# Layer 1's elu as max(min(exp(h), 1), h + 1), with h + 1 from the product with W, in a four-layer graph kernel planned by a list scheduler

## Chip, cores, metric

One core of a Trainium2 chip. The jobs ran on several chips, so each kernel is compared with the kernel before on the same chip. The metric is device microseconds of an execution, the median of several. Each run also has a profile of one execution. Ratios are computed as the mean time of one kernel's runs over the mean of the other's runs of the same rounds, so they are not quite the ratio of the medians that are quoted.

## The reference, cut to what matters

`x` is 64 x 256 x 128 in fp32, `adj` a 256 x 256 matrix of zeros and ones that all graphs share. Four graph layers follow one another, each as `x = layernorm(x + layer(x))`. The change is in the last line of layer 1:

```python
def _L1_gnn_ref(x, adj, W, a_src, a_dst):
    h = jnp.einsum('bnf,fo->bno', x, W)
    ...                                   # attention weights attn from h, a_src, a_dst, adj
    h_prime = jnp.einsum('bij,bjo->bio', attn, h)
    return jax.nn.elu(h_prime)            # h if h > 0, else exp(h) - 1
...
x = _layernorm(x + _L1_gnn_ref(...), axis=-1)
```

Layer 2 is a gated recurrence of five steps and holds most of the matmuls.

## The kernel before

The kernel works on 32 units of two graphs each; seven are under way at a time, in seven "lanes" of buffers. Every instruction is first a task in a plan: engine, planned nanoseconds, a function that issues it, the cells it reads and writes. A list scheduler then simulates the five engines with the planned durations and fixes one order for every engine; the program issues that order, with semaphores between the engines. In the trace of the kernel before, the source lines of TensorE, VectorE and ScalarE follow one another as in the built program (1079, 2310 and 1033 stretches of equal lines).

```python
LATENCY = {"pe": 700, "dve": 600, "act": 600, "pool": 700, "sp": 4000}
...
add(DVE, 230, lambda: nc.vector.tensor_copy(wx1.ap[:, 0:D], ps_w1.ap[:, 0:D]), (ps_w1,), (wx1,))
add(DVE, 60, lambda: nc.vector.memset(wx1.ap[:, D : D + 1], 1.0 / D), (), (wx1,))
... # layer 1, per unit; hp is the product divided by the softmax sums, 128 x 512
add(DVE, 330, lambda: nc.vector.tensor_scalar_min(hn.ap, hp.ap, 0.0), (hp,), (hn,))
add(ACT, 550, lambda: nc.scalar.activation(th.ap, hn.ap, AF.Tanh, scale=0.5), (hn,), (th,))
add(ACT, 550, lambda: nc.scalar.activation(exf, hn.ap, AF.Exp), (hn,), (ex,))
xf = X[u].ap.rearrange("p b c d -> p (b c d)")
add(DVE, 600, lambda: nc.vector.scalar_tensor_tensor(hp.ap, hp.ap, 0.0, xf, op0=ALU.max, op1=ALU.add),
    (hp, X[u]), (hp,))
add(DVE, 600, lambda: nc.vector.scalar_tensor_tensor(th.ap, exf, 1.0, th.ap, op0=ALU.add, op1=ALU.mult),
    (ex, th), (th,))
add(DVE, 600, lambda: nc.vector.tensor_add(hp.ap, hp.ap, th.ap), (hp, th), (hp,))
layernorm(u, L, y_pairs(hp))
```

It computes exp(m) - 1, with m = min(h, 0), as (exp(m) + 1) * tanh(m / 2): three VectorE operations of 512 columns, one cheaper minimum and two ScalarE functions per unit.

The softmax here doesn't subtract the row's maximum and nothing guards it: scores larger than these inputs give would overflow.

## Time and profile before

| | before |
|---|---|
| median of 3 runs | 1464.49 us (1464.2 to 1466.8) |
| profiled span | 1463.0 us |
| TensorE busy | 1431.2 us, 98% |
| VectorE busy | 1101.1 us, 75% |
| ScalarE busy | 723.2 us, 49% |

TensorE's line is the one that bounds; the others are read for what they make TensorE wait for. The prediction below shows the lines themselves.

To see where TensorE loses time I also use a number that the page does not print. In an unbroken stream at full clock successive matmuls of this trace start 0.429 us apart at 512 columns, 0.216 us at 256 and 0.109 to 0.114 us at 128 to 133; at half clock, the 256-column ones start 0.427 us apart. Each start-to-start distance in the trace, less this pitch, is **lost time**: waits, half clock, and the many small hitches that "busy" hides. The pitches of all 5733 matmuls add up to 1415.9 us; the rest of a span is lost time (about 44 us) and the 2.8 us before the first matmul.

### The profile page before, as it was taken

The numbers are of one execution on the slowest core, as the hardware profiler recorded it, in microseconds if no ns is written. First come the engines' busy times: TensorE is split into PE (matmuls) and PEld (weight loads), VectorE is DVE, ScalarE is ACT, GpSimd is POOL, SyncE is SP. The second block draws the span as 40 slices with busy tenths as digits, with TensorE's granted clock in tenths as the row PEclk, the third lists the DMA queues.
The fourth block names the chain that finished last, engine by engine and source line by source line (L and its number), as shares of the span: only waits on it lengthen the run. The fifth ranks groups of instructions, "written<-read, shape, count | busy, mean of one in ns | idle before, by whom it ended". The sixth has DMA issues, their size and how long they took to land.

```text
span 1463.0 us, 18345 instructions
## 1 busy us (share of the span) xinstructions
PE 1431.2 (98%) x5733; PEld 967.9 (66%) x5733; DVE 1101.1 (75%) x2569; ACT 723.2 (49%) x1372; POOL 146.2 (10%) x134
## 2 busy tenths in 40 slices
PE   7899999999999999999999999999999999999998
PEld 6666666666667766577666666676666766665667
DVE  6884778868769788777886778977976877767565
ACT  4664446446354465444554545535554554544431
POOL 0110101100011101001010011111100100001011
PEclk9899999999999999999999999999999999999999
DMA  6211243453534444534435344344343334443212
GB/s 148 46 37 22 65 96 86 95 110 78 116 80 95 104 98 87 118 74 99 104 80 108 78 109 100 84 92 107 72 98 85 89 89 99 93 101 70 46 44 65
DMA packets 495280, 126.90 MB, mean 87 GB/s; under 512 B 443856, under 2 KB 465104, under 8 KB 495184
## 3 DMA queue, kind: packets, MB, share of 16 engines
q1 hardware_dynamic: 495184, 125.73, 38.7%
q8 instruction: 46, 0.75, 0.2%
q14 instruction: 50, 0.41, 0.1%
HBM read 71.41 MB, written 54.25 MB: 86 GB/s over the span
## 4 chain that ended last, share of the span: by engine, by line
PE 93%; DVE 3%; ACT 2%; DMA 1%; issue 0%; SPq 0%; DVEq 0%; ACTq 0%
PE ps L678 45%; PE ps L658 22%; PE ps L747 8%; PE ps L754 4%; PE ps L620 3%; PE ps L590 3%; PE ps L523 2%; PE ps L634 2%; PE ps L585 2%; PE ps L721 1%; ACT e L609 1%; PE ps L430 0%; DVE e L554 0%; DVE st L483 0%; DMA rowu<-cu 0%
## 5 line engine op out<-in xcount | busy, mean ns | idle before, releaser
L678 PE MATMUL ps<-m,gT 128*128 128x512 f32 x960 | 460.9, 593 | 3.6 <-ACT m L674 3.6
L678 PEld LDWEIGHTS ps<-m,gT 128*128 128x128 f32 x960 | 177.7, 190 | 152.8 <-issue 126.4
L488 POOL TENSOR_TENSOR rstd<-ve,nhalf 128x4 f32<-128x4 f32 x128 | 145.5, 1139 | 1311.5 <-DVE ve L485 1268.9
L658 PE MATMUL ps<-adjTp,ht 128*128 128x256 f32 x928 | 231.7, 381 | 1.8 <-DMA ht<-hb 1.5
L658 PEld LDWEIGHTS ps<-adjTp,ht 128*128 128x128 f32 x928 | 174.5, 191 | 74.4 <-issue 50.1
L697 DVE TENSOR_TENSOR p<-p,xT 128x512 f32<-128x512 f32 x160 | 109.6, 686 | 95.3 <-ACT p L691 95.0
L674 ACT COPY m<-ps 128x512 f32<-128x512 f32 x160 | 93.4, 584 | 174.0 <-PE ps L658 170.1
L684 ACT ACTIVATE e<-ps,bias 128x512 f32<-128x512 f32 x160 | 109.8, 686 | 133.9 <-PE ps L678 133.8
L693 ACT ACTIVATE e<-ps,bias 128x512 f32<-128x512 f32 x160 | 109.7, 686 | 117.0 <-PE ps L678 116.7
L678 PE MATMUL ps<-xT,gT 128*128 128x512 f32 x320 | 161.4, 594 | 3.1 <-DVE xT L700 3.1
L686 DVE SCALAR_TENSOR_TENSOR e<-e,xT 128x512 f32<-128x512 f32 x160 | 109.2, 684 | 72.4 <-ACT e L684 70.9
L678 PE MATMUL ps<-e,u5T 128*128 128x512 f32 x320 | 161.9, 592 | 0.0
L691 ACT ACTIVATE p<-ps,bias 128x512 f32<-128x512 f32 x160 | 109.7, 686 | 77.9 <-PE ps L678 74.0
L658 PE MATMUL ps<-adjT,x 128*128 128x256 f32 x512 | 132.2, 383 | 0.0
L658 PEld LDWEIGHTS ps<-adjT,x 128*128 128x128 f32 x512 | 95.8, 192 | 42.6 <-issue 32.0
L698 DVE SCALAR_TENSOR_TENSOR p<-e,p 128x512 f32<-128x512 f32 x160 | 109.5, 685 | 2.8 <-ACT e L693 0.4
L700 DVE SCALAR_TENSOR_TENSOR xT<-p,xT 128x512 f32<-128x512 f32 x160 | 109.5, 685 | 2.0
L483 DVE BATCH_NORM_STATS2 st<-ps 128x6 f32<-128x256 f32 x128 | 53.7, 426 | 57.5 <-PE ps L754 38.9
L678 PEld LDWEIGHTS ps<-e,u5T 128*128 128x128 f32 x320 | 59.2, 190 | 51.1 <-issue 40.7
L609 ACT ACTIVATE e<-m,esd 128x256 f32<-128x256 f32 x120 | 87.0, 761 | 2.1 <-DMA m<-row 2.1
L678 PEld LDWEIGHTS ps<-xT,gT 128*128 128x128 f32 x320 | 59.1, 190 | 41.8 <-issue 31.0
L708 DVE STREAM_TRANSPOSE p<-xT 128x512 f32<-128x512 f32 x116 | 81.6, 705 | 1.4
(135 smaller groups left out, 1861.2 us busy)
## 6 DMA issues: line engine op xcount, KB each, us to landing
hb<-p SPq DMA_DIRECT2D x174, 256.0 KB, 2.1
ht<-hb SPq DMA_DIRECT2D x464, 64.0 KB, 2.5
m<-row SPq DMA_DIRECT2D x60, 256.0 KB, 3.7
xT<-hb SPq DMA_DIRECT2D x232, 64.0 KB, 2.5
out_dram<-x SPq DMA_DIRECT2D x32, 256.0 KB, 2.4
z<-in_x_dram SPq DMA_DIRECT2D x100, 64.0 KB, 2.4
z<-in_x_dram SPq DMA_DIRECT2D x7, 256.0 KB, 4.2
u<-rowu SPq DMA_DIRECT2D x60, 3.8 KB, 3.0
```

The source lines that it names most:

```text
L488: add(POOL, 1050, lambda: nc.gpsimd.tensor_tensor(rstd.ap, ve.ap, nhalf.ap, op=ALU.pow), (ve, nhalf), (rstd,))
L609: add(ACT, 600, lambda g=g, b=b: nc.scalar.activation(e.ap[:, g, :].rearrange("p (c n) -> p c n", c=NC), ev()[:, b], AF.Prelu, bias=esd.ap ...
L658: add(PE, mm_ns(N), lambda b=b, mc=mc: nc.tensor.matmul(ps.ap[:, b * N : (b + 1) * N], lhs(b, mc), mat.ap[:, mc, :], start=(mc == 0), stop ...
L678: add(PE, mm_ns(T), lambda: nc.tensor.matmul(ps.ap, w(), rhs.ap, start=start, stop=stop, skip_group_check=True), (c, rhs), (ps,))
L684: add(ACT, 600, lambda ps_g=ps_g: nc.scalar.activation(r.ap, ps_g.ap, AF.Tanh, bias=bias2.ap[:, 1:2], scale=0.5), (ps_g, bias2), (r,))
L686: add(DVE, 600, lambda h=h: nc.vector.scalar_tensor_tensor(r.ap, r.ap, 1.0, h.ap, op0=ALU.add, op1=ALU.mult), (r, h), (r,))
L691: add(ACT, 600, lambda ps_v=ps_v: nc.scalar.activation(v.ap, ps_v.ap, AF.Tanh, bias=bias2.ap[:, 2:3]), (ps_v, bias2), (v,))
L693: add(ACT, 600, lambda ps_g=ps_g: nc.scalar.activation(z.ap, ps_g.ap, AF.Tanh, bias=bias2.ap[:, 0:1], scale=0.5), (ps_g, bias2), (z,))
L697: add(DVE, 600, lambda h=h: nc.vector.tensor_sub(v.ap, v.ap, h.ap), (v, h), (v,))
L698: add(DVE, 600, lambda: nc.vector.scalar_tensor_tensor(v.ap, z.ap, 1.0, v.ap, op0=ALU.add, op1=ALU.mult), (v, z), (v,))
L700: add(DVE, 600, lambda h=h, new=new: nc.vector.scalar_tensor_tensor(new.ap, v.ap, 0.5, h.ap, op0=ALU.mult, op1=ALU.add), (v, h), (new,))
L747: add(PE, mm_ns(N), lambda k=k, src=src, c=c, b=b: nc.tensor.matmul(view(c)[:, :, b, :], bn(src.ap)[:, b, c * P : (c + 1) * P], w3.ap[:, k ...
```

## The change

Write h for the value that goes into the elu (h_prime in the reference). The product with W that makes h gets 1/D added to every entry of W. The rows of layer 1's input sum to D there (the kernel already adds 1 to each element of the normalized input), so the product, divided by the softmax sums, is h + 1 without an instruction more, and `hp` holds it. The exp takes off the 1 again with a bias of -1. Then elu(h) + 1 = max(min(exp(h), 1), h + 1), and the 1 left over drops out in the layernorm that follows. Per unit one VectorE minimum, one VectorE 512-wide operation and one ScalarE tanh go.

```diff
+    minus1 = cell("minus1", [P, 1])
+    add(DVE, 60, lambda: nc.vector.memset(minus1.ap, -1.0), (), (minus1,))
...
-    add(DVE, 230, lambda: nc.vector.tensor_copy(wx1.ap[:, 0:D], ps_w1.ap[:, 0:D]), (ps_w1,), (wx1,))
+    add(DVE, 230, lambda: nc.vector.tensor_scalar_add(wx1.ap[:, 0:D], ps_w1.ap[:, 0:D], 1.0 / D), (ps_w1,), (wx1,))
...
-        add(DVE, 330, lambda: nc.vector.tensor_scalar_min(hn.ap, hp.ap, 0.0), (hp,), (hn,))
-        add(ACT, 550, lambda: nc.scalar.activation(th.ap, hn.ap, AF.Tanh, scale=0.5), (hn,), (th,))
-        add(ACT, 550, lambda: nc.scalar.activation(exf, hn.ap, AF.Exp), (hn,), (ex,))
+        add(ACT, 550, lambda: nc.scalar.activation(exf, hp.ap, AF.Exp, bias=minus1.ap), (hp, minus1), (ex,))
         xf = X[u].ap.rearrange("p b c d -> p (b c d)")
-        add(DVE, 600, lambda: nc.vector.scalar_tensor_tensor(hp.ap, hp.ap, 0.0, xf, op0=ALU.max, op1=ALU.add),
-            (hp, X[u]), (hp,))
-        add(DVE, 600, lambda: nc.vector.scalar_tensor_tensor(th.ap, exf, 1.0, th.ap, op0=ALU.add, op1=ALU.mult),
-            (ex, th), (th,))
-        add(DVE, 600, lambda: nc.vector.tensor_add(hp.ap, hp.ap, th.ap), (hp, th), (hp,))
+        add(DVE, 600, lambda: nc.vector.scalar_tensor_tensor(hp.ap, exf, 1.0, hp.ap, op0=ALU.min, op1=ALU.max),
+            (ex, hp), (hp,))
+        add(DVE, 600, lambda: nc.vector.tensor_add(hp.ap, hp.ap, xf), (hp, X[u]), (hp,))
```

The list scheduler sees fewer tasks, and from about 57 us on every engine's queue has another order.

More of the change, by code (lines that the diff above doesn't have):

```diff
@@ L623, in layer1 @@
         add(ACT, 500, lambda: nc.scalar.copy(px.ap, ps_x.ap), (ps_x,), (px,))
-        rs, hp, hn, th = L["rs"], L["ht"], L["m"], L["xT1"]
+        rs, hp = L["rs"], L["ht"]
         ex = L["h0"]
```

## The prediction

> **What bounds the kernel now.** I read the page's busy table first, then its slices, then the waits of TensorE, then 2 us windows of the first 90 us, then VectorE's and TensorE's timelines where TensorE stood still.
>
> The busy table and the slices (one digit is the busy tenths of 1/40 of the span):
> ```profile
> PE 1431.2 (98%) x5733; PEld 967.9 (66%) x5733; DVE 1101.1 (75%) x2569; ACT 723.2 (49%) x1372; POOL 146.2 (10%) x134
> ...
> PE   7899999999999999999999999999999999999998
> ...
> PEclk9899999999999999999999999999999999999999
> ```
> TensorE is busy 98% of 1463.0 us and every slice but the first two and the last is at 9. Busy alone could hide slack[...], so I checked the pace: the chain has 8 matmuls of L678 in 3.43 us, 429 ns each for 512 columns, and 16 of L658 in 3.45 us, 216 ns for 256. The same 0.84 ns a column from both sizes is a stream without gaps. The change does not remove a matmul, so nothing below 1431 us is in reach, and at most 1463.0 - 1431.2 = 31.8 us (2.2%) is to be had, from TensorE's idle time. Where that lies, from the waits of TensorE:
> ```profile
> PE ps L430 <- DVE x L497: 4.7, 1, 4.7
> PE ps L473 <- DVE esd L595: 4.2, 2, 3.2
> PE ps L678 <- ACT m L674: 3.6, 3, 1.8
> PE ps L678 <- DVE xT L700: 3.1, 2, 1.9
> ...
> PE ps L620 <- DVE p L613: 2.2, 1, 2.2
> PE ps L658 <- DMA ht<-hb: 1.5, 2, 1.3
> ```
> The columns are total, times and longest, in us. By time: 4.4 us waiting for the first loads, 11.5 us between 28 and 57 us (the first units' layers 0 and 1, with too few units under way to fill TensorE), 9.0 us in eight short waits of at most 1.9 us from 212 to 1229 us, and about 6.7 us after the last matmul. Layer 1's elu lies ahead of the longest one, L430 <- L497: L430 transposes unit 0's layer-1 output, L497 writes it. In 2 us windows (busy us of PE, PEld, DVE, ACT, POOL, then granted clock):
> ```profile
> 50.00:52.00 2.00, 2.00 (x20) 1.99 (x18) 2.00 (x7) 0.78 (x4) 1.01 (x1) 1.00 0.00 0
> 52.00:54.00 2.00, 0.19 (x2) 0.00 (x0) 2.00 (x8) 1.15 (x2) 0.03 (x1) 1.00 0.00 0
> 54.00:56.00 2.00, 0.00 (x0) 0.00 (x0) 2.00 (x9) 0.00 (x0) 0.98 (x1) 0.55 0.04 1
> 56.00:58.00 2.00, 1.16 (x4) 0.88 (x5) 2.00 (x8) 0.00 (x0) 0.00 (x0) 0.50 0.04 12
> 58.00:60.00 2.00, 2.00 (x7) 1.52 (x6) 2.00 (x9) 0.00 (x0) 1.82 (x2) 0.50 0.38 119
> 60.00:62.00 2.00, 2.00 (x12) 1.78 (x11) 2.00 (x10) 1.22 (x3) 0.30 (x1) 0.74 0.02 4
> ```
> Here VectorE, full in every window, is the bound; TensorE stands idle from 52.2 to 56.8 us and then runs at half clock until about 61 us.
>
> [...]after 4.65 us of idleness the clock was 0.50, and L658 pairs took 1.06 us in place of 0.60; the 1.9 us waits later left it at 1.00. [...]the trace has 681 to 688 ns on L646, L648 and L650, whatever the operations are, so a min with a max in one instruction should cost the same.[...]
>
> **The change part by part.** The layer-1 group rows of before:
> ```profile
> L646 DVE SCALAR_TENSOR_TENSOR ht<-ht,x 128x512 f32<-128x512 f32 x32 | 22.0, 687 | 0.5
> L648 DVE SCALAR_TENSOR_TENSOR xT<-h,xT 128x512 f32<-128x512 f32 x32 | 21.8, 682 | 1.3 <-ACT h L644 1.1
> L650 DVE TENSOR_TENSOR ht<-ht,xT 128x512 f32<-128x512 f32 x32 | 21.8, 681 | 0.3
> ...
> L642 DVE TENSOR_SCALAR m<-ht 128x512 f32<-128x512 f32 x32 | 13.5, 422 | 0.5
> ...
> L643 ACT ACTIVATE xT<-m 128x512 f32<-128x512 f32 x32 | 20.1, 627 | 15.7 <-DVE m L642 15.5
> L644 ACT ACTIVATE h<-m 128x512 f32<-128x512 f32 x32 | 19.8, 618 | 0.0
> ```
> There are 32 units. *VectorE* loses the min (13.5 us) and one of three 512-wide operations (21.8 us): 35.3 us, so about 1066 us busy. *ScalarE* loses the tanh (20.1 us)[...]: net -17 us, about 706 us. *TensorE* keeps the same matmuls. The added constant is one 60 ns memset; the added scalar in the weight's copy rides on a copy already there. So some 52 us of work goes, but from engines at 75% and 49%, beside a TensorE at 98%: over most of the span it is worth nothing.
>
> What is on the path is the start. Units 0 and 1 both pass through layer 1 there on the full VectorE, and in issue spacing the removed pair costs 0.33 + 0.62 = 0.95 us per unit. The shorter chain also moves the list scheduler's order, which can be compared without running. On TensorE the order is identical up to unit 3's layer-0 matmuls; then, before, came unit 0's transposes (waiting at 52.2 us), while after has all 24 layer-0 matmuls of unit 4 (8 of L585's kind, 16 of L590's) ahead of them. On VectorE the elu, statistics and norm of unit 0 come in fewer instructions. I laid after's VectorE order out with before's spacings, from row L554 at 47.09 us: two adds, two statistics, max-min (about 50.0), add (50.7), two statistics with unit 1's pieces between (51.8), variance (52.2), 1.1 us of POOL's power beside unit 3's statistics and unit 4's scaling (53.7), unit 1's max-min (54.3), first normalized piece 54.7 to 54.9. Before it came at 56.78: about 1.9 us earlier. For TensorE:
> - At 52.2 it can do L585 of unit 4 (0.89 us), waits about 0.6 us for unit 4's scaled h, does L590 (1.75 us) to about 55.5. These 2.64 us were done later before, behind the gap.
> - Unit 0's transposes then find most of their inputs ready. [...]the clock stays full: of 4.2 us of work at half clock, 2.1 us come back.
> - Small waits are left: 0.6 us above, about 0.4 us among the pieces, about 1.2 us until ScalarE has copied m and xT for the first L678, 2.2 to 2.4 us together, where 4.65 us stood.
> Sum: 4.65 - 2.3 = 2.35 us, and 2.1 us of clock: 4.4 us. VectorE stays near full until 68 us and may give a little back as a later wait, so I take 4 us.
>
> Elsewhere: the last 60 TensorE rows have the same shape (the same two units end together) and no layer 1, so the 6.7 us tail and the 4.4 us of loads stay. The earlier waits (L473, L620: 6.4 us) come before any elu and stay too. The eight short waits, 9.0 us, will be reshuffled, since the whole order from 57 us on differs; with VectorE 3% emptier I would sooner see 7 to 9 us than more, but where an in-order queue stalls is chance: 0, give or take 4 us. Total 1464.5 - 4.5 = 1460.
>
> **The rivals.** (1) *Fully hidden*: the start gap fills, but VectorE, full from 32 to 68 us, gives it back a few us later; then 1463 to 1465. For it speaks VectorE's saturation in those windows; against it, that the removed work is itself VectorE's, in that stretch, and that the cold clock vanishes whatever comes later. (2) *The lighter vector engines pay everywhere*: each of 32 units' chains is shorter by an instruction pair and a hop, and the short mid-run waits nearly vanish: 4 + 7 us, 1453 to 1454. For it, three of those waits name VectorE's L700 or lie where layer 1 runs (212 to 227 us); against it, the others name ScalarE's m or a DMA, and lie in layer 2. (3) *The new order is worse*: the schedule is made from planned durations, and a reshuffled queue gets more short waits or a second cold spell (each cold spell costs its gap and some 2 us): 1467 to 1472. Nothing in the profile speaks for it but that the order is not fitted to real durations. A bound by VectorE or ScalarE is ruled out: both lose work.
>
> **Range and chances.** The centre is 1460; rivals 1 and 2 sit 4 to 6 us either side, and rival 3 has a smaller weight: 1454 to 1466 for 8 in 10. Faster by over 2% needs under 1435 us, nearly all idle time gone, with tail and loads left untouched: 1%. Slower by over 2% needs 29 us of new waits: 1%. Within 2%: 98%.
>
> **What would show it.** Right: VectorE near 1066 us, ScalarE near 706, TensorE's matmul count unchanged; the L430 <- L497 wait of 4.7 us down to under 1.5; clock 1.00 from 52 to 62 us; idle total near 27 us; tail still 6 to 7 us. The half-clock spell at 35 to 44 us should still stand. Wrong if [...]mid-run waits leave 5 to 13 us (step: reshuffle is neutral), or if the operations that remain take longer than 690 ns each.

The forecast's sum came to 1464.5 - 4.5 = 1460 us. In ScalarE's, the term for a longer exp is cut; with it the tanh's 20.1 us became 17. That the clock would stay full in the filled start, which gives 2.1 us of the sum, was the estimate.

## The result, and the profile after

The changed kernel took 1465.34 us median (1464.17 to 1467.01, 4 runs) against 1465.47 us before (4 runs): ratio 1.000, 95% interval 0.998 to 1.002. The profiled span went from 1463.0 to 1462.4 us. A repeat of both on another chip gave 0.9989 (0.9977 to 1.0001) for the changed kernel. Some 32 us of VectorE's work and 17 us of ScalarE's are gone, and the time is about the same.

The page after: busy table and slices.

```profile
PE 1431.6 (98%) x5733; PEld 966.1 (66%) x5733; DVE 1069.5 (73%) x2506; ACT 706.2 (48%) x1340; POOL 142.6 (10%) x134
...
PE   7899999999999999999999999999999999999998
```

The elu's groups after (count, busy us, mean ns, idle before):

```profile
L649 DVE TENSOR_TENSOR ht<-ht,x 128x512 f32<-128x512 f32 x32 | 21.9, 685 | 0.4
L647 DVE SCALAR_TENSOR_TENSOR ht<-h,ht 128x512 f32<-128x512 f32 x32 | 21.9, 685 | 9.5 <-ACT h L645 9.4
...
L645 ACT ACTIVATE h<-ht,minus 128x512 f32<-128x512 f32 x32 | 23.1, 721 | 24.0 <-DVE ht L642 24.0
```

Minimum with maximum in one instruction costs 685 ns, as the other operations with two 512-wide tensors here do (681 to 687 ns before).

The start, in the same 2 us windows and columns as the prediction's:

```profile
50.00:52.00 2.00, 2.00 (x20) 2.00 (x20) 2.00 (x6) 1.06 (x5) 0.00 (x0) 1.00 0.37 74
52.00:54.00 2.00, 1.78 (x16) 1.59 (x15) 2.00 (x10) 0.72 (x1) 0.90 (x1) 1.00 0.00 0
54.00:56.00 2.00, 1.50 (x13) 1.53 (x14) 2.00 (x6) 0.00 (x0) 2.00 (x3) 1.00 0.00 0
56.00:58.00 2.00, 2.00 (x15) 1.70 (x14) 2.00 (x11) 0.00 (x0) 1.26 (x2) 1.00 0.00 0
58.00:60.00 2.00, 1.70 (x7) 0.82 (x6) 2.00 (x11) 1.07 (x2) 0.57 (x1) 1.00 0.04 1
60.00:62.00 2.00, 2.00 (x7) 0.97 (x6) 2.00 (x10) 0.00 (x0) 0.66 (x1) 1.00 0.47 50
```

The hole of 4.65 us is filled and the clock stays at 1.00. The start gained what was hoped for. But the waits of TensorE after:

```profile
PE ps L677 <- ACT m L673: 4.7, 7, 1.8
PE ps L476 <- DVE esd L598: 4.2, 2, 3.2
...
PE ps L657 <- DVE x L496: 2.5, 1, 2.5
...
PE ps L677 <- DMA xT<-hb: 1.2, 1, 1.2
```

The wait of L430's kind (a transpose of unit 0's output) is gone, the earlier one of L476 stands as it did, and in mid-run there are new ones: L673's seven waits in place of three, and one of 2.5 us at 315 us for a normalization on VectorE (L496). Lost time by stretch (us), for both traces of each kernel:

| | to 40 | 40 to 75 | 75 to 1400 | after 1400 | sum |
|---|---|---|---|---|---|
| before | 14.2 | 8.8 | 14.4 | 6.8 | 44.2 |
| before, again | 15.2 | 11.3 | 14.4 | 6.8 | 47.8 |
| after | 14.9 | 4.6 | 17.2 | 6.8 | 43.6 |
| after, again | 14.5 | 5.5 | 18.5 | 6.8 | 45.4 |

40 to 75 us gained 4.2 and 5.8 us; 75 to 1400 us lost 2.8 and 4.1 us. A further sign that the prediction had named, an idle total near 27 us, did not come: 1462.4 - 1431.6 = 30.8 us. The question is whether the mid-run loss belongs to the work or to the order of the queues.

### The profile page after: what moved, and what is told of

It is laid out like the page before. It is cut to its first block, busy times and chain, and to the rows that moved or that the text cites. A ratio compares the mean times of both kernels' runs of the same rounds, so it can differ in the third digit from the quotient of the medians.

```text
span 1462.4 us, 18213 instructions
## 1 busy us (share of the span) xinstructions
PE 1431.6 (98%) x5733; PEld 966.1 (66%) x5733; DVE 1069.5 (73%) x2506; ACT 706.2 (48%) x1340; POOL 142.6 (10%) x134
## 4 chain that ended last, share of the span: by engine, by line
PE 90%; DVE 5%; ACT 4%; DMA 1%; SPq 0%; issue 0%; POOL 0%; DVEq 0%; ACTq 0%
PE ps L677 44%; PE ps L657 21%; PE ps L746 8%; PE ps L753 4%; PE ps L623 3%; PE ps L593 3%; PE ps L637 2%; PE ps L526 2%; PE ps L588 1%; PE ps L720 1%; ACT e L612 1%; DMA m<-row 1%; DVE st L486 1%; DVE e L557 1%; ACT p L571 0%; DVE x L500 0%
## 5 line engine op out<-in xcount | busy, mean ns | idle before, releaser
L677 PE MATMUL ps<-m,gT 128*128 128x512 f32 x960 | 462.7, 594 | 5.4 <-ACT m L673 4.7
L677 PEld LDWEIGHTS ps<-m,gT 128*128 128x128 f32 x960 | 177.6, 190 | 150.2 <-issue 125.1
L491 POOL TENSOR_TENSOR rstd<-ve,nhalf 128x4 f32<-128x4 f32 x128 | 141.9, 1112 | 1314.4 <-DVE ve L488 1197.6
L657 PE MATMUL ps<-adjTp,ht 128*128 128x256 f32 x928 | 228.8, 380 | 2.8 <-DVE x L496 2.5
L657 PEld LDWEIGHTS ps<-adjTp,ht 128*128 128x128 f32 x928 | 173.7, 190 | 74.8 <-issue 50.2
L673 ACT COPY m<-ps 128x512 f32<-128x512 f32 x160 | 93.2, 584 | 177.7 <-PE ps L657 171.9
L677 PE MATMUL ps<-xT,gT 128*128 128x512 f32 x320 | 162.3, 594 | 2.2 <-DMA xT<-hb 1.2
L677 PE MATMUL ps<-e,u5T 128*128 128x512 f32 x320 | 162.2, 593 | 0.3 <-DVE e L685 0.3
L657 PE MATMUL ps<-adjT,x 128*128 128x256 f32 x512 | 130.5, 379 | 0.0
L657 PEld LDWEIGHTS ps<-adjT,x 128*128 128x128 f32 x512 | 94.7, 190 | 42.1 <-issue 30.7
L677 PEld LDWEIGHTS ps<-e,u5T 128*128 128x128 f32 x320 | 59.4, 190 | 53.9 <-issue 44.1
L677 PEld LDWEIGHTS ps<-xT,gT 128*128 128x128 f32 x320 | 58.7, 190 | 43.7 <-issue 27.1
```

The lines of the kernel that those rows point to most:

```text
L491: add(POOL, 1050, lambda: nc.gpsimd.tensor_tensor(rstd.ap, ve.ap, nhalf.ap, op=ALU.pow), (ve, nhalf), (rstd,))
L657: add(PE, mm_ns(N), lambda b=b, mc=mc: nc.tensor.matmul(ps.ap[:, b * N : (b + 1) * N], lhs(b, mc), mat.ap[:, mc, :], start=(mc == 0), stop ...
L677: add(PE, mm_ns(T), lambda: nc.tensor.matmul(ps.ap, w(), rhs.ap, start=start, stop=stop, skip_group_check=True), (c, rhs), (ps,))
```

## The experiments

The theories. **A:** the start gained about 4 us, and the new order, not the arithmetic, lost it again in mid-run. **B:** VectorE, full in the start, gives back whatever it gains, in any order. **C:** the removed work is worth something in mid-run too. Because the plan is ordinary code, work and order can be parted: a task may stay in the plan and issue nothing, or issue more than it is planned for. In each such kernel TensorE's order was compared instruction by instruction with that of the kernel it copies, and was identical. The diffs are shortened.

### Short elu in the old order

```diff
+        add(DVE, 330, lambda: None, (hp,), (hn,))                      # was min
+        add(ACT, 550, lambda: None, (hn,), (th,))                      # was tanh
+        add(ACT, 550, lambda: nc.scalar.activation(exf, hp.ap, AF.Exp, bias=minus1.ap), (hn,), (ex,))
+        add(DVE, 600, lambda: None, (hp, X[u]), (hp,))                 # was max, add
+        add(DVE, 600, ... min, max as in the change ..., (ex, th), (th,))
+        add(DVE, 600, lambda: nc.vector.tensor_add(hp.ap, hp.ap, xf), (hp, th), (hp,))
```

> The short elu of the changed kernel, issued in the order of the kernel before: the planner still places the three removed instructions, which then issue nothing. TensorE's order was compared and is identical to before. Theory A (the start gained about 4 us, and the new order then lost it again in waits between 75 and 400 us that belong to the order, not to the arithmetic): the waits of TensorE after 75 us stay as before (9 us in some eight waits, of the same lines and at the same places, to within 2 us); in the start the first normalized piece of unit 0 comes about 1 us earlier, TensorE's gap there is about 3.7 us in place of 4.65, and the clock still falls to half. So 1 to 2 us below before. Theory B (VectorE, full in the start, gives back whatever it gains whatever the order): same as before within 1 us, with new waits on VectorE between 60 and 100 us. Theory C (the removed work was worth something all along): more than 4 us below before, mid-run waits under 5 us.

Measured: 1464.18 us median (5 runs) against 1467.47 before (11 runs), ratio 0.9977 (0.9965 to 0.9989): 3.4 us faster. It lies between the 1 to 2 us of theory A and the over 4 us of theory C. The gap in the start is as expected, and the clock fell to half at 56.4 us (0.60 between 56 and 58 us; PE's timeline; in brackets the idle time before the row):

```profile
57.90 0.48 PE L431 MATMUL ps<-ident,x 128*128 128x128 f32 x1 [3.75 <-DVE x L498]
```

Lost time: 15.4, 9.4, 12.4, 6.8 us in the four stretches. The mid-run waits are those of before, at the same places, with one difference worth 2 us. Before, near 716 us (columns as in the windows above; the clock is third from the end):

```profile
714.00:716.00 2.00, 0.16 (x1) 0.19 (x2) 2.00 (x8) 0.73 (x2) 1.25 (x1) 1.00 0.26 40
716.00:718.00 2.00, 2.00 (x5) 1.07 (x5) 2.00 (x11) 0.00 (x0) 0.00 (x0) 0.60 0.00 0
718.00:720.00 2.00, 2.00 (x7) 1.61 (x6) 2.00 (x7) 0.00 (x0) 0.00 (x0) 0.55 0.04 1
```

The same place with the short elu:

```profile
716.00:718.00 2.00, 0.84 (x2) 0.49 (x3) 2.00 (x8) 0.32 (x2) 0.97 (x1) 1.00 0.17 27
718.00:720.00 2.00, 2.00 (x10) 1.70 (x9) 2.00 (x10) 0.00 (x0) 0.00 (x0) 1.00 0.04 1
```

Before, a wait of 1.93 us for VectorE was followed by half clock for 3.4 us (716.40 to 719.81 us); with VectorE's queue a little shorter the wait is 1.65 us and the clock stays at 1.00. Of the two kernels below that split the units, the one with a wait of 1.96 us here has the half clock too (0.50 from 720 to 722 us), and the one with 1.65 us does not (1.00 from 710 to 724 us). So the work is worth something in mid-run as well, which theory A left out. Theory B is refuted: in a fixed order the short elu is faster.

### Long elu in the new order

The min and tanh ride in the slot of the exp, the extra VectorE operation in that of the min-max; so VectorE's own order is only nearly that of the changed kernel.

```diff
-        add(ACT, 550, lambda: nc.scalar.activation(exf, hp.ap, AF.Exp, bias=minus1.ap), (hp, minus1), (ex,))
+        add(ACT, 550, lambda: (min into hn, tanh of hn into th, exp of hn into exf), (hp, minus1), (ex,))
-        add(DVE, 600, lambda: min-max, (ex, hp), (hp,))
+        add(DVE, 600, lambda: (max-add into hp, add-mult into th), (ex, hp), (hp,))
```

> The long elu of the kernel before, issued in the order of the changed kernel (the extra instructions ride in the slots of the ones that are planned). TensorE's order was compared and is identical to the changed kernel's. Theory A: the waits after 75 us look like the changed kernel's (10 to 11 us, among them one of about 2.5 us near 315 us), and the start keeps most of its gain, as unit 4's matmuls still fill the gap and the clock stays up, but unit 0's pieces come 1 to 2 us later than in the changed kernel: 1 to 3 us above the changed kernel. Theory B: the same as before and changed, within 1 us. Theory C: 4 us or more above the changed kernel, with more waits spread over the whole run.

Measured: 1471.13 us, ratio 1.0026 (1.0013 to 1.0039) to before: the same elu, in the new order, is 3.8 us slower than in the old. Lost time 14.7, 7.1, 22.4, 6.8 us. The 2.5 us wait near 315 us is there again, and the longer queue made another one longer (PE's timeline; the changed kernel has 0.30 us at this L657 matmul, near 199 us):

```profile
202.77 3.25 PE L660 MATMUL ps<-adjTp,ht 128*128 128x256 f32 x8 [1.79 <-ACT h L529]
```

By its matmuls, the clock fell to half after the second: these eight took 3.25 us, where eight of that size at full clock, L623 at 222.63 us, took 1.89. What the clock did near 315 us is not shown. Its mid-run was expected like the changed kernel's, and is 4 to 5 us worse: again the work counts there. The start was to keep the clock up and did not: after a wait of 2.42 us, from 56.13 us, the 16 matmuls of L593 took 3.39 us, where 16 at 50.86 us had taken 1.95.

### Short elu in units 0 and 1 only, and in the other 30 only

Both in the old order. Where the long load is wanted, the three removed instructions are issued with their sizes and their results unused.

```diff
+        light = u < 2          # the other kernel: light = u >= 2
+        add(DVE, 330, lambda: None if light else nc.vector.tensor_scalar_min(hn.ap, hp.ap, 0.0), (hp,), (hn,))
+        add(ACT, 550, lambda: None if light else nc.scalar.activation(th.ap, hn.ap, AF.Tanh, scale=0.5), (hn,), (th,))
...
+        add(DVE, 600, lambda: None if light else nc.vector.scalar_tensor_tensor(
+            L["r"].ap, hp.ap, 0.0, xf, op0=ALU.max, op1=ALU.add), (hp, X[u]), (hp,))
```

> Order of before, the short elu in units 0 and 1 only; for the other 30 units the three removed instructions are issued again with the same sizes, their results unused. Theory A and the prediction's step that the removed work matters only in the start: the same as the short elu everywhere in that order, within 1 us. Theory C: as slow as before, and slower than the short elu everywhere by most of its gain.

> Order of before, the long load in units 0 and 1 and the short elu in the other 30. If only the start matters: the same as before within 1 us, although 33 us of VectorE's and 16 us of ScalarE's work is gone. If the work in mid-run matters (Theory C): 2 us or more below before.

Measured: first two only 0.9986 (0.9975 to 0.9998), 2 us faster; the other 30 only 0.9981 (0.9969 to 0.9992), 2.8 us faster. Mid-run lost time is 14.6 us in the first, with the half clock after the 1.96 us wait, and 12.4 us in the second, without it (wait of 1.65 us). In the start, TensorE's wait for unit 0 is 3.75 us in the first and 5.49 us in the second. The lost time from 40 to 75 us does not show this gain (10.6 and 10.3 us), and the first one's trace is of its slowest run, so the start's part rests on the shorter wait and on the times, whose interval ends just under 1. With that said, the start and the mid-run each give a part, and the prediction's sentence that over most of the span the work is worth nothing is wrong by some 2 us. The two ratios are 0.0005 apart and their intervals 0.0023 wide, so which part is larger stays open. The planned waits differ a little from the long elu's: here the exp does not wait for the minimum, so the load is the long one's and the chain is not.

### Both kernels again

> The kernel before, unchanged, for a second trace and for the spread. All theories: ratio 1.000 within 0.001. The waits that belong to the order come again at the same lines (L678 after m and xT, 6 to 8 us in all; L430 after L497 near 4.7 us); what differs is the start-up up to 20 us (the first trace lost 5.0 us there, all four other traces so far 6.2 to 7.1), so 1 to 2 us of the difference between the two first traces is load timing, not the change.

> The changed kernel, unchanged, on the same chip as the rest. From the two by two of the last job: short elu is worth 3.4 us in the old order, the new order costs the long elu 3.8 us. If arithmetic and order add up (Theory A), the changed kernel comes out at 0.999 to 1.001 of before, and 3 to 4 us above the short elu in the old order. If they do not add up (the new order only suits or hurts one of them), it lies more than 2 us away from before. Waits: 2.5 us near 315 us and 1.2 us near 218 us again.

Measured: before 0.9994 (0.9982 to 1.0006), changed 0.9989 (0.9977 to 1.0001). The mid-run waits of before, from its second trace:

```profile
PE ps L678 <- ACT m L674: 3.6, 3, 1.8
PE ps L678 <- DVE xT L700: 3.1, 2, 1.9
PE ps L658 <- DMA ht<-hb: 1.6, 2, 1.4
```

These are the first trace's to within 0.1 us: an order's mid-run waits come again. The start's did not: the wait of L430 was expected near 4.7 us and was 5.55 us. What does not come again in mid-run is the clock after the waits. The same 2.46 us wait of the changed kernel at 315 us, first trace:

```profile
314.00:316.00 2.00, 1.09 (x5) 0.99 (x6) 1.82 (x8) 0.00 (x0) 1.11 (x2) 1.00 0.04 1
316.00:318.00 2.00, 2.00 (x11) 1.77 (x10) 1.39 (x4) 0.59 (x1) 0.00 (x0) 1.00 0.37 68
```

and second trace:

```profile
314.00:316.00 2.00, 1.00 (x2) 0.84 (x3) 1.74 (x8) 0.00 (x0) 1.21 (x2) 0.67 0.04 1
316.00:318.00 2.00, 2.00 (x6) 1.63 (x5) 1.48 (x4) 0.00 (x0) 0.00 (x0) 0.50 0.36 62
```

One wait, one length, once at full clock afterwards and once at half: 1.3 us of difference in the mid-run between two executions of one kernel. The traces of the two first kernels show more. In that of before, the clock changes at 9.84, 33.73, 43.97, 54.21, 61.04, 716.40, 719.81 and 1460.50 us: 7, 3, 3, 2, 192, 1 and 217 times 3.413 us apart. In that of the changed kernel it changes at 12.94, 36.83, 43.66 and 1460.19 us: 7, 2 and 415 times. Counted in such periods, the two traces have 841 at full clock. Six of them were followed by half clock, and in each of the six TensorE, by its busy times in the trace, was idle for at least 0.565 of the period; in the other 835 it was idle for at most 0.535. The 2.46 us wait was cut in two by these periods in the first trace of the changed kernel (0.86 and 1.60 us, at most 0.469 of a period idle). In the second, the 0.67 between 314 and 316 us puts the fall of the clock at 314.68 us, so that 2.14 us of the wait, 0.63 of a period, lay in the 3.413 us before it. So in these traces the share of one period that a wait fills parts the two cases, and its length alone does not. The wait at 716 us, 1.93 us in before, lay in one period, idle for 0.565 of it; the 1.96 us, with the fall at 720.0 us, did too (0.57); 1.65 us is 0.48 of a period at most. How often such a wait is cut in two, and what the clock does then, no run shows, so the 2 us there belong to executions like the two whose windows show the fall. With the start, whose loss differs by 3.5 us between the two traces of before, this is enough for most of the spread of some 4 us within each kernel. Another expectation failed: the changed kernel was to lie 3 to 4 us above the short elu in the old order. By the ratios, 0.9989 and 0.9977, it lies 1.8 us above, and their intervals overlap.

### Other orders of the same instructions

To see whether the original pair of orders is typical, both kernels were planned with other numbers. First, 220 in place of 110 ns for a TensorE transpose. The author read two matmuls of 0.108 us for one transpose in the trace; it has one matmul for each (176 for the 176 of L721, in fours that start 0.109 us apart), so 220 ns is just another number:

```diff
-            add(PE, 110, lambda g=g: nc.tensor.transpose(...), (src, ident), (ps,))      # six such places
+            add(PE, 220, lambda g=g: nc.tensor.transpose(...), (src, ident), (ps,))
```

> The kernel before, planned with 220 ns in place of 110 ns for a transpose on TensorE[...]. Same instructions, another order. Theory A (orders are a lottery of a few us that no step of the change aims at): a time anywhere from 1458 to 1475 us, differing from before by 2 us or more as likely as not, by waits after 75 us. If orders hardly matter: within 1 us of before.

> The changed kernel planned with 220 ns for a transpose. Theory A: its difference from the kernel before under the same planning is about -3.5 us plus chance of some 4 us, so from -8 to +1 us, not the same 0 as under the first planning. Rival (the shorter chain makes any order of the planner worse by what it saves): 0 within 1 us again.

Second, a longer latency after VectorE and ScalarE:

```diff
-    LATENCY = {"pe": 700, "dve": 600, "act": 600, "pool": 700, "sp": 4000}
+    LATENCY = {"pe": 700, "dve": 700, "act": 700, "pool": 700, "sp": 4000}
```

> The kernel before, planned with 700 ns in place of 600 ns from the end of an instruction of VectorE or ScalarE to its use elsewhere: another order of the same instructions. Lottery: within 8 us either side of before, not within 1 us.

> The changed kernel under the same other planning. Lottery: -3.5 us and chance of some 5 us against the long elu planned so, so -9 to +2 us. If a shorter chain gave the planner a worse order by rule, as at first sight in the original pair: 0 within 1 us.

And the two mixed kernels of the first planning, made as those above:

> Transposes planned at 220 ns; the short elu in the order that this planning gives the long one (TensorE's order compared: identical). If arithmetic is worth about 3.5 us in any order and the rest of the 16 us between the pair is order: 3 to 6 us below the long elu in this order (1474.5), so 1468 to 1472; cold spells after short waits may add or take 2 us each. If the short elu itself were worth the 16 us: near 1458.5.

> Transposes planned at 220 ns; the long elu in the order that this planning gives the short one (TensorE's order compared: identical). Arithmetic 3.5 us, rest order: 1461 to 1465, still below the kernel before (1467.4) although it carries the whole long elu. If the short elu itself were worth the 16 us: near 1474.

Measured, as ratios to the kernel before on the same chip, with the 95% interval, the median, and lost time from 75 to 1400 us:

| order planned | elu | ratio | median us | mid-run lost us |
|---|---|---|---|---|
| original, for the long elu | long | 1 | 1467.1 to 1467.5 | 14.4 |
| original, for the long elu | short | 0.9977 (0.9965 to 0.9989) | 1464.18 | 12.4 |
| original, for the short elu | long | 1.0026 (1.0013 to 1.0039) | 1471.13 | 22.4 |
| original, for the short elu | short | 0.9989 (0.9977 to 1.0001) | 1465.61 | 17.2, 18.5 |
| 220 ns, for the long elu | long | 1.0056 (1.0043 to 1.0069) | 1474.49 | 19.0 |
| 220 ns, for the long elu | short | 1.0003 (0.9990 to 1.0015) | 1467.10 | 12.4 |
| 220 ns, for the short elu | long | 0.9987 (0.9973 to 1.0001) | 1464.56 | 11.8 |
| 220 ns, for the short elu | short | 0.9942 (0.9930 to 0.9954) | 1458.45 | 7.2 |
| latency 700, for the long elu | long | 1.0015 (1.0003 to 1.0028) | 1468.58 | 15.6 |
| latency 700, for the short elu | short | 0.9952 (0.9940 to 0.9965) | 1459.82 | 9.9 |

In a fixed order the short elu is worth 0.0023, 0.0037, 0.0053 and 0.0045 of the time, 3.4 to 7.8 us, always faster. The first is one ratio with its interval; the others are differences of two ratios from two chips, each uncertain by about 0.0018 (an estimate from the intervals). The order is worth as much: under the original planning, the new order costs the long elu 3.8 us and the short elu 1.8 us, the latter not clear of the noise (its traces have 5 to 6 us more lost in mid-run, and 4 to 5 us less in the start); under the 220 ns planning it gains 10 us and 9 us. Taken together, which is how the change is made, the difference is -1.6 us or none (original), -17 us and -9 us. Without the mixed kernels one would have called the change worth nothing, or 17 us. The 17 us were not expected either: 8 us less to 1 us more had been said for the pair under 220 ns.

Where a fixed order gives more than the start explains, the waits show it. The 220 ns order for the long elu, with the long elu (PE's timeline):

```profile
218.82 2.07 PE L678 MATMUL ps<-xT,gT 128*128 128x512 f32 x2 [3.83 <-DVE xT L700]
261.75 1.13 PE L678 MATMUL ps<-m,gT 128*128 128x512 f32 x2 [2.77 <-ACT e L684]
```

and with the short elu, the same two places:

```profile
219.01 1.81 PE L680 MATMUL ps<-xT,gT 128*128 128x512 f32 x2 [3.83 <-DVE xT L702]
260.11 1.13 PE L680 MATMUL ps<-m,gT 128*128 128x512 f32 x2 [1.24 <-ACT e L686]
```

The first wait did not move, the second was more than halved, and with it went a stretch at half clock (eight 256-column matmuls from 263.30 us took 3.43 us in the first, from 261.50 us 1.89 in the second). The same holds near 539 us: after 1.79 us the next eight of that size took 2.81 us, after 0.83 us 1.89. Each wait has its own chain, and only some of those run through an elu.

The short elu planned with 220 ns has the lowest time found, 8.5 us below before (0.9942), and is correct; the interval of the one planned with latency 700 overlaps. For the short elu, one number in the planner did more (0.0047, 7 us) than the change itself had done under the original planning. That 220 ns is the true duration the trace does not show (0.109 us, above), and for the long elu the same number cost 8 us.

## Why the prediction was right or wrong

The time was inside the range, by under 1 us at its upper end, and the class was right; the centre was 5 us low. The range held partly by luck: the start's gain came as forecast and a loss that was not forecast cancelled it. Two slips of the sum: it takes 4 us for the start and then subtracts 4.5, and by their own numbers rival 1 lies 3 to 5 us and rival 2 6 to 7 us from the centre, not 4 to 6.

- **TensorE bounds, at most 2% to be had:** right. The number of matmuls and the tail (6.8 or 6.9 us of lost time in every trace) are unchanged.
- **VectorE 1066 us, ScalarE 706 us:** 1069.5 and 706.2. For VectorE the sum of 35.3 us counted full durations, though neighbours overlap (before, L648 takes 0.68 us from 50.41 us, and the next instruction starts at 51.01); the issue spacing, which the text had as well, 32 x 0.95 = 30.4 us, is nearer to the 31.6 us that went. The exp took 721 ns with its bias operand, 618 before without: 103 ns or 3.3 us over 32 units, a little more than the term cut above.
- **The start:** right, with its mechanism. Unit 4's matmuls fill the gap, the wait in front of L593 is 0.72 us (0.6 predicted), that before L677 0.30 us (1.2), one of 0.73 us at 64.75 us was not foreseen. Predicted gain 4.4 us; lost time fell by 4.2 us in the first pair of traces and 5.8 in the second. The mixed kernels divide it: the short elu alone, in the old order, left a gap of 3.75 us and the half clock.
- **Rival 1, VectorE gives it back at once:** refuted in that form; 57 to 75 us lost 1.9 us in the first trace of both kernels. Its time, 1463 to 1465 us, was nearly met, for another reason.
- **Rival 2, the work pays everywhere:** right in kind once the order is held fixed (3.4 to 7.8 us). **Rival 3, the new order is worse:** right in kind for the mid-run; the start's gain hid it in the time.
- **"0, give or take 4 us" for the mid-run waits:** the step that made the centre wrong. It was 2.8 to 4.1 us, inside its margin and of the wrong sign for the centre: the text leaned to fewer waits. It is the sum of two terms that the prediction lumped together: in that stretch the new order costs some 5 to 8 us (12.4 to 17.2 or 18.5 with the short elu, 14.4 to 22.4 with the long one), and the removed work gives back 2 to 5 us (14.4 to 12.4 in the old order, 22.4 to 17.2 or 18.5 in the new).
- **"Over most of the span it is worth nothing":** wrong by 2 us in the old order and by more in the others.
- **"The 1.9 us waits later left it at 1.00":** a misreading. The clock was 0.60 and 0.55 between 716 and 720 us; the 200 us window showed it as 0.99. Nor did the fall come after the 4.65 us wait: before the transposes the clock fell at 54.2 us, 2.0 us into it, in the text's own window of 0.55. That the clock stayed full in the changed start was right; in the first trace no period of 3.413 us between 50 and 75 us was idle for more than 0.19.
- **The base:** 1464.5 us from three runs is lower than most that came later: on three other chips 11, 11 and 9 runs had medians of 1467.47, 1467.38 and 1467.11 us, though five more on one of these had 1465.6. Chance or chip stays open.

## What to carry to other kernels

When a planner fixes the queues from planned durations, a change in any task is two changes, one of work and one of order; keep the tasks in the plan and issue nothing (or issue more than is planned) to time them apart before judging either. On a kernel whose bound engine is 98% busy, read the remaining 2% one wait at a time, with the clock in windows of 2 us around each: here a wait of 1.93 us was followed by 3.4 us at half clock, which cost about 1.7 us more (an estimate: half of the 3.4), and one wait of 2.46 us was followed by half clock in one trace and by full clock in another. So compare several executions, or the waits themselves, before calling a difference of 2 us an effect of the change. If orders are worth several microseconds, a few replannings with other numbers are cheap trials and may beat the change itself.
